# Four graph layers on one core: where the edges' order is checked, and how the edges are loaded

## The chip, the cores and the metric

The kernel runs on one core of a Trainium2 chip. A core has a matrix engine (TensorE, PE in the profile), a vector engine (VectorE, DVE), a scalar engine (ScalarE, ACT), GpSimd (POOL) and SyncE (SP), which work side by side, each through its own list of instructions in order. DMAs are issued from the lists of SP, ACT and POOL and carried out by 16 DMA engines. The metric is the device time of one execution in microseconds (us), as the median of several runs. One execution was also taken by the hardware profiler; its span and rows are what this text reads.

## The reference, cut to what matters

The graph has 3125 nodes with 128 features and 53,125 edges, given as `src`, `dst` and two edge types. Four layers follow each other, each with a residual and a layer norm:

```python
x = layernorm(x + L0(x, src, dst))                   # GIN, four times:  h = x + segment_sum(x[src], dst); relu(h@W1+b1)@W2+b2
x = layernorm(x + L1(x, src, dst, edge_type_8))      # a mean per relation
x = layernorm(x + L2(x, src, dst, edge_type_16))     # with attention per relation
x = layernorm(x + L3(x, src, dst, edge_type_8))      # gated
```

`setup_inputs` sorts the edges by `dst`. The reference itself does not depend on their order.

## The kernel before

**Two paths.** `any_order` is right for edges in any order. `in_order` is quicker and right only where the edges are sorted by `dst` and the destinations advance about evenly. `gnn_kernel` checks that first, and branches: `in_order` in the If, `any_order` in the Else.

**The edges as tiles.** 128 edges make a tile; there are TE = 416 tiles, the last with 5 edges. `gnn_kernel` loads each of the four edge arrays into a `raw` tile of 104 partitions (QR) by 4 by 128: partition q holds the tiles q, 104+q, 208+q and 312+q. Each array takes three DMAs: a first of 104 rows by three pieces of 512 bytes (L1170), a second of 103 rows of 512 bytes (L1171), and the five last edges (L1172). `dst` and `edge_type_8` are issued from SP, `src` and `edge_type_16` from ACT. Then two DMAs of single numbers fetch each tile's first and last destination (`lohi`, L1178 to L1180).

**The check and the places.** VectorE turns the arrays into floats (L1190), computes the tests (`bad`, `inner`, L1194 to L1217), and two small matmuls sum them to `flag` (L1219 to L1221). Then it computes, for each edge, where it belongs: `mod` (the source within its block of 128) and `kb` (block and destination, together), with `rel`, `k8` and the types for later layers. TensorE transposes seven such arrays (L1241), so that a tile becomes a column of 128 partitions; they are copied out of PSUM (L1242) and stored to DRAM as `keys` and `srcs` (L1245 to L1247). All engines then wait and branch on `flag` (L1248, L1250).

**The build of the adjacency matrix.** `gin_layers` loads `keys` back as `places` (L642), prepares the rows `offs` and `sto` (L654 to L662), and runs over the 416 tiles (L665). In each, VectorE makes two one-hot matrices `ohs` and `ohk` (L673, L675), TensorE multiplies them into the PSUM tile `pa` (L677, and L681 for the columns that the tile before left open), and ScalarE writes the result into `AT` in bf16 (L684). `pa` has three buffers, `ohs` four, `ohk` three. Each group of 8 tiles reads its offsets into registers first.

**What runs beside the build.** `first_parts(j)`, for j = 0 to 6, is called at the tiles 5, 14, ... 59 (L670). It loads 512 rows of `x` into `xn`, which has one buffer, and splits them into three bf16 parts `xs` on ScalarE and VectorE (`split`, L546). `dense(0, j)` multiplies `xs` with 512 columns of `AT` as soon as these are done (first after tile 73): one step of it, two matmuls, is run behind each tile (L685). After the build come the three further GIN steps, then layers 1 to 3, whose `edges` are loaded from `keys` at L694.

**What sets the order.** The order within an engine is made at build time by a scheduler that walks the program with modelled durations: an instruction keeps the rank of its place in the program, but a later one that its model finds ready while the engine is free goes ahead. On the chip each engine then keeps that order.

Of the kernel before, what the change touches and what calls it, by code (L numbers as in the profile page):

```python
# [21 lines left out]
F32 = mybir.dt.float32  # L22
# [7 lines left out]
P = 128  # L30
# [30 lines left out]
DRIFT = 40.0  # L61
PADDST = 4095
# [451 lines left out]
def gin_layers(ctx: ExitStack, tc: tile.TileContext, a: dict, pre: dict, outer: ExitStack, eps, srcI, xtab):  # L514
# [5 lines left out]
    ident, keys, lo, hi = (pre[k] for k in ("ident", "keys", "lo", "hi"))  # L520
# [3 lines left out]
    wk = ctx.enter_context(tc.tile_pool(name="g_wk", bufs=1, side="right"))  # L524
    xsd = [dram.tile([NP, 3, D], BF16, name=f"xsd{l}") for l in range(NL - 1)]

    AT = big.tile([P, NB, N + W], BF16, name="AT")

    xs = [big.tile([P, BPB if j < NCH - 1 else NB - BPB * (NCH - 1), 3, D], BF16, name=f"xs{j}") for j in range(NCH)]
    nc.vector.memset(xs[NCH - 1], 0.0)  # L530
    b1 = wk.tile([P, NL], F32, name="b1")
    with nc.allow_non_contiguous_dma(reason="a few columns"):
        nc.scalar.dma_start(b1, a["L0_gnn_b1"].rearrange("l o -> o l"))
# [85 lines left out]
    sp_pool = sp_ctx.enter_context(tc.tile_pool(name="g_parts", bufs=1, side="right"))  # L619
# [19 lines left out]
    weights(0)  # L639
    with tc.tile_pool(name="g_build", bufs=1) as bp, tc.tile_pool(name="g_hot", bufs=4) as hots:  # L640
        places = bp.tile([P, 2, TE], F32, name="places")
        nc.sync.dma_start(places, keys[:, :2, :])  # L642
        srcmod, keyb = places[:, 0, :], places[:, 1, :]
        nc.scalar.dma_start(srcI, pre["srcs"][:, :])
        iotah = bp.tile([P, NK], F16, name="iotah")
        nc.gpsimd.iota(iotah, pattern=[[1, NK]], base=0, channel_multiplier=0, allow_small_or_imprecise_dtypes=True)
        identh = bp.tile([P, P], BF16, name="identh")
        nc.vector.tensor_copy(identh, ident)


        regs = bp.tile([33, TE], I32, name="regs")
        row = bp.tile([1, TE], F32, name="row")
        offs, sto = regs[0:1, :], regs[32:33, :]
        nc.vector.tensor_copy(offs, lo)  # L654
        nc.vector.memset(row, 0.0)
        nc.vector.tensor_sub(row[:, 1:], hi[:, :FULL], lo[:, :FULL])
        nc.vector.tensor_scalar(row[:, 1:], row[:, 1:], -float(W), None, op0=OP.add)
        same = bp.tile([1, TE], F32, name="same")
        nc.vector.memset(same, 0.0)
        nc.vector.tensor_tensor(same[:, 1:], lo[:, 1:], hi[:, :FULL], OP.is_equal)  # L660
        nc.vector.tensor_tensor(row, row, same, OP.mult)
        nc.vector.tensor_scalar(sto, row, float(W), None, op0=OP.add)  # L662
        old = None
        under = []
        for t in range(TE):  # L665
# [4 lines left out]
            if t % 9 == 5 and t // 9 < NCH:  # L670
                first_parts(t // 9)
# [16 lines left out]
            for j in range(NCH):  # L688
                if t == last_tile(cols(j)[1]):
                    add_self(j)  # L690
                    under.append(dense(0, j, keep))
    ep = outer.enter_context(tc.tile_pool(name="f_edges", bufs=1))
    edges = ep.tile([P, 4, TE], F32, name="edges")
    nc.scalar.dma_start(edges, keys[:, 2:, :])  # L694
# [453 lines left out]
def gnn_kernel(ctx: ExitStack, tc: tile.TileContext, a: dict, out: bass.AP):  # L1148
    nc = tc.nc
    pp = ctx.enter_context(tc.tile_pool(name="pre", bufs=1))  # L1150
    dram = ctx.enter_context(tc.tile_pool(name="pre_dram", bufs=1, space=bass.MemoryType.DRAM))
    R8 = a["L1_gnn_W"].shape[0]
    keys = dram.tile([P, 6, TE], F32, name="keys")
    srcs = dram.tile([P, TE], I32, name="srcs")
    lo = pp.tile([1, TE], F32, name="lo")
    hi = pp.tile([1, TE], F32, name="hi")
    flag = pp.tile([1, 1], I32, name="flag")
    ident = pp.tile([P, P], F32, name="p_ident")
    iota = pp.tile([P, 2 * P], F32, name="p_iota")
    ones = pp.tile([P, P], F32, name="p_ones")  # L1160
    with (tc.tile_pool(name="pre_psum", bufs=1, space=bass.MemoryType.PSUM) as psum,
          tc.tile_pool(name="pre_tmp", bufs=1) as tmp):

        raw = {}
        for n, (name, pad) in enumerate((("dst", PADDST), ("src", 0), ("edge_type_8", 0), ("edge_type_16", 0))):
            eng = (nc.sync, nc.scalar)[n % 2]
            r = raw[name] = tmp.tile([QR, 4, P], I32, name="raw_" + name)
            nc.vector.memset(r[96:QR, 3, :], pad)
            e = a[name]
            eng.dma_start(r[:, :3, :], e[:3 * QR * P].rearrange("(k q p) -> q k p", q=QR, p=P))  # L1170
            eng.dma_start(r[:QR - 1, 3, :], e[3 * QR * P:FULL * P].rearrange("(q p) -> q p", p=P))  # L1171
            eng.dma_start(r[QR - 1:QR, 3, :LASTN], e[FULL * P:].rearrange("(q p) -> q p", q=1))  # L1172
        lohi = tmp.tile([1, 2, TE], I32, name="lohi")
        e = a["dst"]
        with nc.allow_non_contiguous_dma(reason="the tiles' first and last destinations"):
            firsts = bass.AP(tensor=e.tensor, offset=e.offset, ap=[[1, 1], [P, TE]])
            lasts = bass.AP(tensor=e.tensor, offset=e.offset + P - 1, ap=[[1, 1], [P, FULL]])
            nc.sync.dma_start(lohi[:, 0, :], firsts)  # L1178
            nc.scalar.dma_start(lohi[:, 1, :FULL], lasts)
            nc.scalar.dma_start(lohi[:, 1, FULL:], e[E - 1:E].rearrange("(a o) -> a o", a=1))  # L1180
        make_identity(nc, ident)
        nc.gpsimd.iota(iota, pattern=[[1, 2 * P]], base=0, channel_multiplier=0,
                       allow_small_or_imprecise_dtypes=True)
        nc.vector.memset(ones, 1.0)


        f = {}
        for name in raw:
            f[name] = tmp.tile([QR, 4, P], F32, name="f_" + name)
            nc.vector.tensor_copy(f[name], raw[name])  # L1190
        nc.vector.tensor_copy(lo, lohi[:, 0, :])
        nc.vector.tensor_copy(hi, lohi[:, 1, :])
        bad = tmp.tile([1, 8, TE], F32, name="bad")
        nc.vector.memset(bad, 0.0)  # L1194
        nc.vector.tensor_tensor(bad[:, 0, :FULL], hi[:, :FULL], lo[:, 1:], OP.is_gt)
        span = tmp.tile([1, TE], F32, name="span")
        nc.vector.tensor_sub(span, hi, lo)
        nc.vector.tensor_scalar(bad[:, 1, :], span, float(W - 1), None, op0=OP.is_gt)
        nc.vector.tensor_scalar(bad[:, 2, :FULL], span[:, :FULL], 1.0, None, op0=OP.is_lt)
        drift = tmp.tile([1, TE], F32, name="drift")  # L1200
        nc.gpsimd.iota(drift, pattern=[[1, TE]], base=0, channel_multiplier=0,
                       allow_small_or_imprecise_dtypes=True)
        nc.vector.scalar_tensor_tensor(drift, drift, -float(N * P) / E, lo, op0=OP.mult, op1=OP.add)
        nc.vector.tensor_scalar(bad[:, 3, :], drift, DRIFT, None, op0=OP.is_gt)
        nc.vector.tensor_scalar(bad[:, 4, :], drift, -DRIFT, None, op0=OP.is_lt)

        step = tmp.tile([1, TE], F32, name="step")
        nc.vector.tensor_sub(step[:, :FULL], lo[:, 1:], lo[:, :FULL])
        nc.vector.tensor_scalar(bad[:, 5, :FULL], step[:, :FULL], float(W), None, op0=OP.is_gt)
        nc.vector.tensor_scalar(bad[:, 6, :1], lo[:, :1], 0.0, None, op0=OP.is_gt)  # L1210
        nc.vector.tensor_scalar(bad[:, 7, :1], lo[:, FULL:], float(N - W), None, op0=OP.is_lt)
        inner = tmp.tile([QR, 4, P - 1], F32, name="inner")
        nc.vector.tensor_tensor(inner, f["dst"][:, :, :P - 1], f["dst"][:, :, 1:], OP.is_gt)
        found = tmp.tile([QR, 1], F32, name="found")
        nc.vector.tensor_reduce(found, inner, AX.XY, OP.add)
        rows = tmp.tile([1, 1], F32, name="rows")
        nc.vector.tensor_reduce(rows, bad, AX.XY, OP.add)  # L1217
        ps = psum.tile([1, 1], F32, name="ps_found")
        nc.tensor.matmul(ps, ones[:QR, 0:1], found, start=True, stop=False)  # L1219
        nc.tensor.matmul(ps, ones[0:1, 0:1], rows, start=False, stop=True)  # L1220
        nc.vector.tensor_scalar(flag, ps, 0.0, None, op0=OP.is_equal)  # L1221


        rel = tmp.tile([QR, 4, P], F32, name="rel")
        nc.vector.tensor_tensor(rel, f["dst"], f["dst"][:, :, 0:1].to_broadcast([QR, 4, P]), OP.subtract)
        sbI = tmp.tile([QR, 4, P], I32, name="sbI")
        nc.vector.tensor_scalar(sbI, raw["src"], 7, None, op0=OP.arith_shift_right)
        sb = tmp.tile([QR, 4, P], F32, name="sb")
        nc.vector.tensor_copy(sb, sbI)
# [50 lines left out]
```

## Time and profile before

| | us |
|---|---|
| median of 3 runs (2367.03 to 2371.94) | 2369.75 |
| the profiled execution | 2367.41 |
| its span | 2365.6 |
| edges loaded, checked and stored, branch taken: ends | 39.2 |
| `places` landed | 43.1 |
| first tile written to `AT` | 45.7 |
| first matmul of `dense(0, 0)` | 111.3 |
| last tile written to `AT` | 344.6 |
| busy over the span: PE, DVE, ACT, POOL | 81%, 50%, 21%, 50% |

The span begins with the first instruction and ends with the last; 1.8 us of the profiled execution lie around it. A share of busy time is a mean over stages that have different limits, so each stage has to be read by itself. The stretch that the change touches is the first 111 us, and a few instructions at the end of the build and of the kernel.

### The profile page before, as it was taken

Reading aid. Unit: us, or ns where it says so; the run is one execution under the profiler, and the core shown is the slowest. Engines: PE = TensorE matmul, PEld = TensorE weight load, DVE = VectorE, ACT = ScalarE, POOL = GpSimd, SP = SyncE. Lnnn points to the kernel's source line nnn. Section 1 sums busy time; section 2 is a strip of 40 time slices with the busy share of each in tenths; the row PEclk is TensorE's granted clock in tenths of the full one; section 3 lists DMA queues with packets and bytes.
Section 4 is the critical chain, followed back from the end, with each engine's and each line's share of the span. In section 5 each row is a group of like instructions: output and inputs, shape, how many; then the busy total and the mean of one; then the engine's idle time right before and its main releaser. Section 6 shows DMA issues by size and latency. Waiting matters only on the chain.

```text
span 2365.6 us, 37283 instructions
## 1 busy us (share of the span) xinstructions
PE 1921.5 (81%) x10848; PEld 1355.3 (57%) x10898; DVE 1172.6 (50%) x4724; ACT 492.3 (21%) x995; POOL 1194.0 (50%) x1259
## 2 busy tenths in 40 slices
PE   2698899999997899989786777777775778777777
PEld 1244344444445777777665666566664566666666
DVE  5677761121224656565554444455443455554554
ACT  1677761011104010000001222222222000000000
POOL 0000000000006777777774777777774777777774
PEclk8588889999995666676665656666665666767666
DMA  2000012020203222222221222222221222222221
GB/s 67 18 8 8 14 31 65 21 66 25 62 25 88 72 60 60 60 59 59 60 59 36 58 59 57 60 59 60 59 60 38 61 62 63 63 64 63 63 63 41
DMA packets 103154, 122.82 MB, mean 52 GB/s; under 512 B 25851, under 2 KB 82472, under 8 KB 102952
## 3 DMA queue, kind: packets, MB, share of 16 engines
q0 software_dynamic: 40000, 83.59, 14.6%
q1 hardware_dynamic: 51006, 28.49, 4.1%
q10 hardware_dynamic: 11946, 8.27, 1.2%
q8 instruction: 100, 1.64, 0.3%
q14 instruction: 102, 0.84, 0.1%
HBM read 104.98 MB, written 15.27 MB: 51 GB/s over the span
## 4 chain that ended last, share of the span: by engine, by line
PE 57%; issue 13%; DMA 12%; POOL 11%; DVE 6%; ACT 2%; DVEq 0%; SPq 0%; POOLq 0%; ACTq 0%
PE acc L595 16%; PE pw L1005 13%; POOL xg L908 11%; PE pm L1029 8%; DMA xg<-fx,f_srcI 6%; PE pc L1013 5%; PE pa L677 4%; PE pr L1050 3%; DMA xg<-gtab,f_srcI 3%; PE pr L603 1%; PE pr L610 1%; DVE sums L1007 1%; PE pa L681 1%; DMA xn<-in_x_dram 1%; DVE ohk L675 1%
## 5 line engine op out<-in xcount | busy, mean ns | idle before, releaser
L908 POOL DMA_INDIRECT xg<-fx,f_srcI x832 | 795.9, 957 | 934.9 <-DMA f_ggb<-in_L_gnn_gate_bias_dram 681.7
L1005 PE MATMUL pw<-oh,xg 128*128 128x128 f32 x2496 | 664.9, 399 | 180.8 <-DMA xg<-fx,f_srcI 83.6
L1005 PEld LDWEIGHTS pw<-oh,xg 128*128 128x128 f32 x2496 | 505.1, 271 | 291.7 <-DVE sums L1007 131.2
L1007 DVE TENSOR_TENSOR sums<-pw,sums 128x128 f32 x1248 | 357.8, 287 | 361.6 <-PE pw L1005 328.7
L908 POOL DMA_INDIRECT xg<-gtab,f_srcI x416 | 394.4, 948 | 151.5 <-issue 104.5
L595 PE MATMUL acc<-AT,xs 128*128 128x512 bf16 (+1 forms) x2050 | 438.2, 355 | 5.2 <-DMA xs<-xsd 1.8
L595 PEld LDWEIGHTS <-xs 128*128 128x128 bf16 x2100 | 176.0, 99 | 197.0 <-issue 19.7
L684 ACT CAST AT<-pa 128x400 f32 x416 | 213.1, 512 | 54.4 <-PE pa L681 28.3
L677 PE MATMUL pa<-ohk,ohs 128*128 128x425 bf16 x416 | 170.4, 424 | 45.7 <-ACT AT L684 18.0
L1013 PE MATMUL pc<-hw,rg 128*8 128x16 f32 x1456 | 92.7, 183 | 95.2 <-DVE rg L985 67.5
L675 DVE TENSOR_SCALAR ohk<-iotah,places 128x425 bf16<-128x425 f16 x416 | 139.2, 335 | 55.6 <-PE pa L681 49.3
L803 ACT COPY sums<-f_zero 128x1024 f32<-128x1024 f32 x74 | 75.2, 1042 | 325.0 <-PE pm L1029 188.0
L1013 PEld LDWEIGHTS pc<-hw,rg 128*8 128x8 f32 x1456 | 65.5, 89 | 129.1 <-DVE rg L985 76.0
L998 DVE SCALAR_TENSOR_TENSOR oh<-f_dcol,edges,coef 128x128 f32<-128x128 f32 x416 | 137.5, 344 | 0.7 <-ACT coef L955 0.6
L1003 DVE TENSOR_SCALAR oh<-p_iota,edges,g 128x128 f32<-128x128 f32 x416 | 135.9, 354 | 0.2
L677 PEld LDWEIGHTS <-ohs 128*128 128x128 bf16 x416 | 42.0, 101 | 139.1 <-DVE ohk L675 88.3
L996 DVE TENSOR_SCALAR oh<-p_iota,edges 128x128 f32<-128x128 f32 x416 | 121.0, 298 | 0.3
L600 DVE COPY hT<-acc 128x512 f32<-128x512 f32 (+1 forms) x28 | 17.3, 619 | 194.2 <-PE acc L595 194.2
L985 DVE TENSOR_TENSOR rg<-h,xg 128x32 f32<-128x32 f32 x104 | 19.8, 190 | 175.9 <-DMA xg<-gtab,f_srcI 170.8
L673 DVE TENSOR_SCALAR ohs<-iotah,places 128x128 bf16<-128x128 f16 x416 | 102.8, 247 | 0.9 <-DMA places<-keys 0.8
L1029 PE MATMUL pm<-f_bases,sums 128*128 128x128 f32 x400 | 100.2, 438 | 0.8 <-DVE sums L1007 0.8
L681 PE MATMUL pa<-ohk,ohs 128*128 x415 | 92.7, 223 | 9.3 <-issue 8.1
(193 smaller groups left out, 1898.5 us busy)
## 6 DMA issues: line engine op xcount, KB each, us to landing
xg<-fx,f_srcI POOLq DMA_INDIRECT x832
xsd<-sp SPq DMA_DIRECT2D x18, 384.0 KB
xg<-gtab,f_srcI POOLq DMA_INDIRECT x416
xs<-xsd SPq DMA_DIRECT2D x9, 384.0 KB
xs<-xsd ACTq DMA_DIRECT2D x9, 384.0 KB
xb<-fx SPq DMA_DIRECT2D x49, 64.0 KB
gtab<-yg SPq DMA_DIRECT2D x25, 68.0 KB
fx<-y SPq DMA_DIRECT2D x25, 64.0 KB
```

What stands on the lines that cost most here:

```text
L595: nc.tensor.matmul(acc[:, :n], xs[s // BPB][:, s % BPB, i, :], AT[:, s, c0:c1], start=s == 0 and i == 0, stop=s == NB - 1 and i == 2)
L675: nc.vector.tensor_scalar(ohk, iotah, keyb[:, t:t + 1], None, op0=OP.is_equal)
L677: nc.tensor.matmul(ps, ohs, ohk, start=True, stop=t == 0)
L684: nc.scalar.copy(AT[:, :, bass.ds(og[t % GRP], W)], ps3[:, :, :W])
L908: nc.gpsimd.indirect_dma_start(out=dst, out_offset=None, in_=table, in_offset=bass.IndirectOffsetOnAxis(ap=idx, axis=0))
L996: nc.vector.tensor_scalar(oh, iota[:, :W * NR], key8[:, u:u + 1], None, op0=OP.is_equal)
L998: nc.vector.scalar_tensor_tensor(oh.rearrange("p (d b) -> p d b", b=NR), W2["dcol"], dlr[:, u:u + 1], cgroups[u - u % GRP][:, u % GRP, :]. ...
L1003: nc.vector.tensor_scalar(oh, iota[:, :W * NR], key8[:, u:u + 1], gate, op0=OP.is_equal, op1=OP.mult)
L1005: nc.tensor.matmul(ps, x[:, u % 4, :D], oh, start=True, stop=True)
L1007: nc.vector.tensor_tensor(w, ps, w, OP.add)
L1013: nc.tensor.matmul(segs[j][:, bass.ds(spot[i][u], W)], r, hw[:, u % GRP, :], start=False, stop=u == last_tile(min(N, (j + 1) * P)))
L1029: nc.tensor.matmul(pb, s[:, r, :], w[:, r, :], start=False, stop=r == NR - 1)
```

## The change

`gnn_kernel` keeps no check of its own. It calls `in_order` without a branch, and at the very end reads `flag`, now the other way round, and runs `any_order` over the output if the edges were not in order:

```diff
-    good = nc.values_load(flag[0:1, 0:1], min_val=0, max_val=1)
-    with tc.If(good > 0) as cmp:
-        in_order(tc, a, out, pre)
-    with cmp.Else():
+    in_order(tc, a, out, pre)
+    bad = nc.values_load(pre["flag"][0:1, 0:1], min_val=0, max_val=1)
+    with tc.If(bad > 0):
         any_order(tc, a, out)
```

The loads and the places move into `gin_layers`. A partition now holds four tiles that follow each other, so an array takes one DMA of 103 rows of 2048 bytes and one of the rest:

```diff
-            nc.vector.memset(r[96:QR, 3, :], pad)
-            eng.dma_start(r[:, :3, :], e[:3 * QR * P].rearrange("(k q p) -> q k p", q=QR, p=P))
-            eng.dma_start(r[:QR - 1, 3, :], e[3 * QR * P:FULL * P].rearrange("(q p) -> q p", p=P))
-            eng.dma_start(r[QR - 1:QR, 3, :LASTN], e[FULL * P:].rearrange("(q p) -> q p", q=1))
+        nc.vector.memset(r[96:QR], pad)
+        rest = E - (QR - 1) * 4 * P
+        flat = r.rearrange("q k p -> q (k p)")
+        eng.dma_start(flat[:QR - 1, :], e[:(QR - 1) * 4 * P].rearrange("(q p) -> q p", q=QR - 1))
+        eng.dma_start(flat[QR - 1:QR, :rest], e[(QR - 1) * 4 * P:].rearrange("(q p) -> q p", q=1))
```

The tiles' first and last destinations are picked out by nine small matmuls with the identity instead of a DMA. Only `kb` and `mod` are transposed before the loop, in the buffers of `pa`, and copied straight into `places`:

```diff
+    def turn(dst, r, copy):
+        pt = psum.tile([P, NK], F32, name="pa", bufs=3)
+        for k in range(4):
+            nc.tensor.transpose(pt[:, k * QR:(k + 1) * QR], r[:, k, :], ident[:QR, :QR])
+        copy(dst.rearrange("p (q k) -> p k q", k=4), pt[:, :TE].rearrange("p (k q) -> p k q", k=4))
...
+    turn(keyb, kb, nc.scalar.copy)
+    turn(srcmod, mod, nc.vector.tensor_copy)
```

The first destinations are clipped to the band that the path can bear (`lo`, `offs`, `sto`), so that the path runs without harm on any edges. The other arrays are turned inside the loop, at the tiles in `LATE`, and stored to DRAM from ACT:

```diff
+LATE = [4, 5, 6, 7, 8, 10]
...
+    def later(i, r):
+        t = tmp.tile([P, TE], F32, name="turned", bufs=2)
+        turn(t, r, nc.scalar.copy)
+        nc.scalar.dma_start(keys[:, i, :], t)
+    def late(i):
+        if i == 0:
+            turn(turnedI, f["src"], nc.vector.tensor_copy)
+            nc.scalar.dma_start(srcs[:, :], turnedI)
+        elif i == 1:
+            later(0, rel)
+        elif i == 2:
+            t8 = fl("edge_type_8", sb)
+            later(3, t8)
+        elif i == 3:
+            nc.vector.scalar_tensor_tensor(mod, rel, float(R8), f["edge_type_8"], op0=OP.mult, op1=OP.add)
+            later(1, mod)
+        elif i == 4:
+            later(2, fl("edge_type_16", kb))
+        elif i == 5:
...
+            nc.vector.tensor_tensor(inner, flat[:, :4 * P - 1], flat[:, 1:], OP.is_gt)
+            nc.vector.tensor_reduce(found, inner, AX.X, OP.add)
+            tmp_ctx.close()
```

(`fl` casts a raw array to float on VectorE, here into the buffers of `sb` and `kb`.) The memory of these arrays is that of `xs` and of the working tiles afterwards. So `room()` makes these at tile 10, with a memset of the last `xs`; `b1`, the first weights and `srcI` are loaded there, and `first_parts` is called at the tiles 23, 32, ... 77:

```diff
-            if t % 9 == 5 and t // 9 < NCH:
-                first_parts(t // 9)
+            if t in LATE:
+                late(LATE.index(t))
+            if t == LATE[-1]:
+                wk = room()
...
+                weights(0)
+                nc.scalar.dma_start(srcI, srcs[:, :])
+            if t > LATE[-1] and t % 9 == 5 and t // 9 - 2 in range(NCH):
+                first_parts(t // 9 - 2)
```

The remaining tests (`checks`: some 20 VectorE instructions on one row of 416 numbers, a reduction and two matmuls into `flag`) stand behind the loop, ahead of the load of `edges`.

More of the change, by code (lines that the diff above doesn't have):

```diff
@@ L519, in gin_layers @@
     NL = a["L0_gnn_W1"].shape[0]
-    ident, keys, lo, hi = (pre[k] for k in ("ident", "keys", "lo", "hi"))
+    R8 = a["L1_gnn_W"].shape[0]
+    ident, iota, ones, flag = (pre[k] for k in ("ident", "iota", "ones", "flag"))
     dram = ctx.enter_context(tc.tile_pool(name="g_dram", bufs=1, space=bass.MemoryType.DRAM))
@@ L523, in gin_layers @@
     big = ctx.enter_context(tc.tile_pool(name="g_big", bufs=1, side="right"))
-    wk = ctx.enter_context(tc.tile_pool(name="g_wk", bufs=1, side="right"))
+    keep_ctx = ExitStack()
+    keep_ = keep_ctx.enter_context(tc.tile_pool(name="g_keep", bufs=1))
     xsd = [dram.tile([NP, 3, D], BF16, name=f"xsd{l}") for l in range(NL - 1)]
+    keys = dram.tile([P, 4, TE], F32, name="keys")
+    srcs = dram.tile([P, TE], I32, name="srcs")
     AT = big.tile([P, NB, N + W], BF16, name="AT")
-    xs = [big.tile([P, BPB if j < NCH - 1 else NB - BPB * (NCH - 1), 3, D], BF16, name=f"xs{j}") for j in range(NCH)]
@@ L530, in gin_layers @@
[L530 to L533, printed above, removed]
+    places = keep_.tile([P, 2, TE], F32, name="places")
+    srcmod, keyb = places[:, 0, :], places[:, 1, :]
+    iotah = keep_.tile([P, NK], F16, name="iotah")
+    identh = keep_.tile([P, P], BF16, name="identh")
+    regs = keep_.tile([33, TE], I32, name="regs")
+    offs, sto = regs[0:1, :], regs[32:33, :]
@@ new lines, in gin_layers @@
+    lo, hi = pre["lo"], pre["hi"]
+    found = keep_.tile([QR, 1], F32, name="found")
+    tmp_ctx = ExitStack()
+    tmp = tmp_ctx.enter_context(tc.tile_pool(name="g_tmp", bufs=1, side="right"))
+    raw, f = {}, {}
+    for n, (name, pad) in enumerate((("dst", PADDST), ("src", 0), ("edge_type_8", 0), ("edge_type_16", 0))):
+        eng = (nc.sync, nc.scalar)[n % 2]
+        r = raw[name] = tmp.tile([QR, 4, P], I32, name="raw_" + name)
+        nc.vector.memset(r[96:QR], pad)
+        e = a[name]
+        rest = E - (QR - 1) * 4 * P
+        flat = r.rearrange("q k p -> q (k p)")
+        eng.dma_start(flat[:QR - 1, :], e[:(QR - 1) * 4 * P].rearrange("(q p) -> q p", q=QR - 1))
+        eng.dma_start(flat[QR - 1:QR, :rest], e[(QR - 1) * 4 * P:].rearrange("(q p) -> q p", q=1))
@@ new lines, in gin_layers @@
+    make_identity(nc, ident)
+    nc.gpsimd.iota(iotah, pattern=[[1, NK]], base=0, channel_multiplier=0, allow_small_or_imprecise_dtypes=True)
+    nc.gpsimd.iota(iota, pattern=[[1, 2 * P]], base=0, channel_multiplier=0, allow_small_or_imprecise_dtypes=True)
+    at = tmp.tile([1, TE], F32, name="at")
+    nc.gpsimd.iota(at, pattern=[[1, TE]], base=0, channel_multiplier=0, allow_small_or_imprecise_dtypes=True)
+    nc.vector.memset(ones, 1.0)
+    def turn(dst, r, copy):
[3 more added lines that the diff above has]
+        copy(dst.rearrange("p (q k) -> p k q", k=4), pt[:, :TE].rearrange("p (k q) -> p k q", k=4))
@@ new lines, in fl @@
+    def fl(name, into=None):
+        f[name] = into if into is not None else tmp.tile([QR, 4, P], F32, name="f_" + name)
+        nc.vector.tensor_copy(f[name], raw[name])
+        return f[name]
+    fl("dst")
+    lohi = psum.tile([P, 2, BANK], F32, name="pr", bufs=1)
+    for i, c in enumerate((0, P - 1)):
+        for k in range(4):
+            m = QR - (i == 1 and k == 3)
+            nc.tensor.matmul(lohi[0:1, i, k * QR:k * QR + m], f["dst"][:, k, c:c + 1], ident[:QR, :m], start=True, stop=True)
@@ new lines, in gin_layers @@
+    nc.tensor.matmul(lohi[0:1, 1, TE - 1:TE], f["dst"][:, 3, LASTN - 1:LASTN], ident[:QR, QR - 1:QR], start=True, stop=True)
+    fl("src")
+    rel = tmp.tile([QR, 4, P], F32, name="rel")
+    nc.vector.tensor_tensor(rel, f["dst"], f["dst"][:, :, 0:1].to_broadcast([QR, 4, P]), OP.subtract)
+    sbI = tmp.tile([QR, 4, P], I32, name="sbI")
+    nc.vector.tensor_scalar(sbI, raw["src"], 7, None, op0=OP.arith_shift_right)
+    sb = tmp.tile([QR, 4, P], F32, name="sb")
+    nc.vector.tensor_copy(sb, sbI)
@@ new lines, in gin_layers @@
+    kb = tmp.tile([QR, 4, P], F32, name="kb")
+    nc.vector.scalar_tensor_tensor(kb, sb, float(WK), rel, op0=OP.mult, op1=OP.add)
+    mod = tmp.tile([QR, 4, P], F32, name="mod")
+    nc.vector.scalar_tensor_tensor(mod, sb, -float(P), f["src"], op0=OP.mult, op1=OP.add)
+    turn(keyb, kb, nc.scalar.copy)
+    turn(srcmod, mod, nc.vector.tensor_copy)
+    nc.vector.tensor_copy(identh, ident)
+    dst0 = keep_.tile([1, 2, TE], F32, name="dst0")
+    for i in range(2):
+        nc.scalar.copy(dst0[:, i, :].rearrange("o (q k) -> o k q", k=4), lohi[0:1, i, :TE].rearrange("o (k q) -> o k q", k=4))
@@ new lines, in gin_layers @@
+    nc.vector.tensor_scalar(at, at, float(N * P) / E, -DRIFT, op0=OP.mult, op1=OP.add)
+    nc.vector.tensor_tensor(lo, dst0[:, 0, :], at, OP.max)
+    nc.vector.tensor_scalar(at, at, 2 * DRIFT, None, op0=OP.add)
+    nc.vector.tensor_tensor(lo, lo, at, OP.min)
+    nc.vector.tensor_scalar(offs, lo, 0.0, float(N - 1), op0=OP.max, op1=OP.min)
+    nc.vector.tensor_copy(lo, offs)
+    nc.scalar.copy(hi, dst0[:, 1, :])
+    row = tmp.tile([1, TE], F32, name="row")
+    nc.vector.memset(row, 0.0)
+    same = tmp.tile([1, TE], F32, name="same")
@@ new lines, in gin_layers @@
+    nc.vector.memset(same, 0.0)
+    nc.vector.tensor_sub(row[:, 1:], hi[:, :FULL], lo[:, :FULL])
+    nc.vector.tensor_scalar(row[:, 1:], row[:, 1:], -float(W), None, op0=OP.add)
+    nc.vector.tensor_tensor(same[:, 1:], lo[:, 1:], hi[:, :FULL], OP.is_equal)
+    nc.vector.tensor_tensor(row, row, same, OP.mult)
+    nc.vector.tensor_scalar(row, row, float(W), 0.0, op0=OP.add, op1=OP.max)
+    nc.vector.tensor_scalar(sto, row, float(W), None, op0=OP.min)
+    def later(i, r):
+        t = tmp.tile([P, TE], F32, name="turned", bufs=2)
+        turn(t, r, nc.scalar.copy)
+        nc.scalar.dma_start(keys[:, i, :], t)
@@ new lines, in gin_layers @@
+    turnedI = tmp.tile([P, TE], I32, name="turnedI")
+    def late(i):
[13 more added lines that the diff above has]
+        elif i == 5:
+            flat = f["dst"].rearrange("q k p -> q (k p)")
+            inner = f["src"].rearrange("q k p -> q (k p)")[:, :4 * P - 1]
+            nc.vector.tensor_tensor(inner, flat[:, :4 * P - 1], flat[:, 1:], OP.is_gt)
+            nc.vector.tensor_reduce(found, inner, AX.X, OP.add)
+            tmp_ctx.close()
@@ new lines, in checks, with add @@
+    def checks(own):
+        first, last = dst0[:, 0, :], dst0[:, 1, :]
+        bad = own.tile([1, TE], F32, name="bad")
+        nc.vector.memset(bad, 0.0)
+        w = own.tile([1, TE], F32, name="bad_w")
+        def add(n, x, bound, op):
+            nc.vector.tensor_scalar(x, x, bound, None, op0=op)
+            nc.vector.tensor_tensor(bad[:, :n], bad[:, :n], x, OP.add)
+        nc.vector.tensor_sub(w[:, :FULL], last[:, :FULL], first[:, 1:])
+        add(FULL, w[:, :FULL], 0.0, OP.is_gt)
+        nc.vector.tensor_sub(w, last, first)
+        add(TE, w, float(W - 1), OP.is_gt)
+        nc.vector.tensor_sub(w, last, first)
+        add(FULL, w[:, :FULL], 1.0, OP.is_lt)
+        nc.vector.tensor_sub(w[:, :FULL], first[:, 1:], first[:, :FULL])
+        add(FULL, w[:, :FULL], float(W), OP.is_gt)
+        nc.vector.tensor_sub(w, first, lo)
+        add(TE, w, 0.0, OP.not_equal)
+        nc.vector.tensor_copy(w[:, 0:1], first[:, 0:1])
+        add(1, w[:, 0:1], 0.0, OP.is_gt)
+        nc.vector.tensor_copy(w[:, 0:1], first[:, FULL:])
+        add(1, w[:, 0:1], float(N - W), OP.is_lt)
+        rows = own.tile([1, 1], F32, name="rows")
+        nc.vector.tensor_reduce(rows, bad, AX.X, OP.add)
+        ps = psum.tile([P, NK], F32, name="pa", bufs=3)
+        nc.tensor.matmul(ps[0:1, 0:1], ones[:QR, 0:1], found, start=True, stop=False)
+        nc.tensor.matmul(ps[0:1, 0:1], ones[0:1, 0:1], rows, start=False, stop=True)
+        nc.vector.tensor_scalar(flag, ps[0:1, 0:1], 0.0, None, op0=OP.is_gt)
@@ L535, in cols, with room @@
+    late_ctx = {}
+    xs = []
+    def room():
+        late_ctx["xs"] = ctx.enter_context(tc.tile_pool(name="g_xs", bufs=1, side="right"))
+        late_ctx["wk"] = ctx.enter_context(tc.tile_pool(name="g_wk", bufs=1, side="right"))
+        xs.extend(late_ctx["xs"].tile([P, BPB if j < NCH - 1 else NB - BPB * (NCH - 1), 3, D], BF16, name=f"xs{j}")
+                  for j in range(NCH))
+        nc.vector.memset(xs[NCH - 1], 0.0)
+        return late_ctx["wk"]
     def cols(j):
@@ L618, in gin_layers @@
     sp_ctx = ExitStack()
-    sp_pool = sp_ctx.enter_context(tc.tile_pool(name="g_parts", bufs=1, side="right"))
     def keep(l, j, pr, rows, nb):
@@ L636, in back @@
                 "(b p) i d -> p b i d", p=rows))
[L639 to L662, printed above, removed]
+    with tc.tile_pool(name="g_hot", bufs=4) as hots:
         old = None
@@ L669, in gin_layers @@
                 sg = values(sto[:, t:t + n], PE, [(0, W)] * n)
-            if t % 9 == 5 and t // 9 < NCH:
-                first_parts(t // 9)
+            if t in LATE:
+                late(LATE.index(t))
+            if t == LATE[-1]:
+                wk = room()
+                b1 = wk.tile([P, NL], F32, name="b1")
+                with nc.allow_non_contiguous_dma(reason="a few columns"):
+                    nc.scalar.dma_start(b1, a["L0_gnn_b1"].rearrange("l o -> o l"))
+                weights(0)
+                nc.scalar.dma_start(srcI, srcs[:, :])
+                sp_pool = sp_ctx.enter_context(tc.tile_pool(name="g_parts", bufs=1, side="right"))
+            if t > LATE[-1] and t % 9 == 5 and t // 9 - 2 in range(NCH):
+                first_parts(t // 9 - 2)
             ohs = hots.tile([P, P], BF16, name="ohs")
@@ L691, in gin_layers @@
                     under.append(dense(0, j, keep))
+    with tc.tile_pool(name="g_checks", bufs=1) as own:
+        checks(own)
+    keep_ctx.close()
     ep = outer.enter_context(tc.tile_pool(name="f_edges", bufs=1))
     edges = ep.tile([P, 4, TE], F32, name="edges")
-    nc.scalar.dma_start(edges, keys[:, 2:, :])
+    nc.scalar.dma_start(edges, keys[:, :, :])
     for stages in under:
@@ L1150, in gnn_kernel @@
     pp = ctx.enter_context(tc.tile_pool(name="pre", bufs=1))
[L1151 to L1167, printed above, removed]
-            nc.vector.memset(r[96:QR, 3, :], pad)
-            e = a[name]
-            eng.dma_start(r[:, :3, :], e[:3 * QR * P].rearrange("(k q p) -> q k p", q=QR, p=P))
-            eng.dma_start(r[:QR - 1, 3, :], e[3 * QR * P:FULL * P].rearrange("(q p) -> q p", p=P))
-            eng.dma_start(r[QR - 1:QR, 3, :LASTN], e[FULL * P:].rearrange("(q p) -> q p", q=1))
[L1173 to L1229, printed above, removed]
-        mod = tmp.tile([QR, 4, P], F32, name="mod")
-        nc.vector.scalar_tensor_tensor(mod, sb, -float(P), f["src"], op0=OP.mult, op1=OP.add)
-        kb = tmp.tile([QR, 4, P], F32, name="kb")
-        nc.vector.scalar_tensor_tensor(kb, sb, float(WK), rel, op0=OP.mult, op1=OP.add)
-        k8 = tmp.tile([QR, 4, P], F32, name="k8")
-        nc.vector.scalar_tensor_tensor(k8, rel, float(R8), f["edge_type_8"], op0=OP.mult, op1=OP.add)
-        turned = tmp.tile([P, 6, TE], F32, name="turned")
-        turnedI = tmp.tile([P, TE], I32, name="turnedI")
-        for n, r in enumerate((mod, kb, f["src"], rel, k8, f["edge_type_16"], f["edge_type_8"])):
-            pt = psum.tile([P, TE], F32, name="pt", bufs=4)
-            for k in range(4):
-                nc.tensor.transpose(pt[:, k * QR:(k + 1) * QR], r[:, k, :], ident[:QR, :QR])
-            (nc.vector.tensor_copy if n % 2 == 0 else nc.scalar.copy)(
-                turnedI if n == 2 else turned[:, n - (n > 2), :], pt)
-            if n == 1:
-                nc.sync.dma_start(keys[:, :2, :], turned[:, :2, :])
-        nc.sync.dma_start(srcs[:, :], turnedI)
-        nc.scalar.dma_start(keys[:, 2:, :], turned[:, 2:, :])
@@ L1248, in gnn_kernel @@
-    good = nc.values_load(flag[0:1, 0:1], min_val=0, max_val=1)
-    pre = {"ident": ident, "iota": iota, "ones": ones, "keys": keys, "srcs": srcs, "lo": lo, "hi": hi}
-    with tc.If(good > 0) as cmp:
-        in_order(tc, a, out, pre)
-    with cmp.Else():
+    pre = {
+        "ident": pp.tile([P, P], F32, name="p_ident"),
+        "iota": pp.tile([P, 2 * P], F32, name="p_iota"),
+        "ones": pp.tile([P, P], F32, name="p_ones"),
+        "lo": pp.tile([1, TE], F32, name="lo"),
+        "hi": pp.tile([1, TE], F32, name="hi"),
+        "flag": pp.tile([1, 1], I32, name="flag"),
+    }
```

## The prediction

> **What bounds the kernel now.** I read the chain of waits over the first 50 us first, because the change rewrites what lies there. Columns: start, length, what.
>
> ```profile
> 1.43 10.98 DMA raw_src<-in_src_dram
> 12.43 5.24 DMA raw_edge_type<-in_edge_type_dram
> ...
> 18.20 0.36 DVE lo L1191
> ...
> 29.92 3.71 PE pt L1241 x20
> ...
> 35.59 3.44 DMA keys<-turned
> 39.34 3.79 DMA places<-keys
> 43.22 0.27 DVE ohs L673
> ```
>
> Three stretches set the start of the build: 17.9 us for the loads, 17.7 us of tests, places and transposes, and 7.6 us for the way to DRAM and back. The first tile reaches `AT` at 45.72.
>
> Second, the windows of the loads, since the change gives them another shape. Columns: stretch, length, busy time of five engines, clock, busy share of the 16 DMA engines, GB/s.
>
> ```profile
> 2.00:3.00 1.00, 0.00 (x0) 0.00 (x0) 0.69 (x1) 0.00 (x0) 0.02 (x1) 1.00 0.73 218
> ...
> 7.00:8.00 1.00, 0.00 (x0) 0.00 (x0) 0.00 (x0) 0.00 (x0) 0.00 (x0) 1.00 0.07 21
> 8.00:9.00 1.00, 0.00 (x0) 0.00 (x0) 0.16 (x1) 0.00 (x0) 0.00 (x0) 1.00 0.07 21
> 9.00:10.00 1.00, 0.00 (x0) 0.00 (x0) 0.27 (x1) 0.00 (x0) 0.00 (x0) 1.00 0.07 20
> ...
> 348.00:349.00 1.00, 1.00 (x7) 0.41 (x5) 0.00 (x0) 0.00 (x0) 0.00 (x0) 1.00 1.01 426
> ```
>
> The pieces of 104 rows (4 x 156 KB) are through by about 6 us. From 6 to 17 us the share is 0.07, one engine of sixteen, at 20 to 21 GB/s: some 0.2 MB, which is the four pieces of 103 rows (4 x 51.5 KB). They landed one after another: the casts started at 8.84, 12.74, 16.31 and 17.86.
>
> Third, what stands beside the early tiles, from the waits (us in total, times, longest):
>
> ```profile
> ACT xs L550 <- DMA xn<-in_x_dram: 27.8, 7, 9.9
> PE pa L677 <- ACT AT L684: 16.0, 9, 3.5
> ```
>
> From 45.2 to 87.1 ScalarE wrote only 32 tiles. Where nothing disturbs it, it writes 8 tiles in 4.58 us (336.21 to 340.79 in the timeline), 0.573 each, 18.3 for 32. So the seven `first_parts` cost 23.6 us. From 111.3 on TensorE is the bound (211.6 busy of 232.8), and everything later follows from when tile 73 is written.
>
> **The change, part by part.**
>
> *The loads.* Each array becomes 103 rows of 2048 B, 210.9 KB. Here a rule speaks against the change. The row first: 103 rows ran on one engine, 104 rows on about twelve (share 0.73). The Trainium skill, "DMA: Bandwidth & Descriptors", section "Why a DMA increments its semaphore by 16 and not by 1", gives the reason: the number of engines is the largest divisor, at most 16, common to the outer sizes of both patterns. 104 gives 13; 103 is prime and gives 1. The same page's rules for kernel authors ask for many small transfers to be joined into large ones; by that alone, on 16 engines at 20.5 GB/s, the four would move in 2.6 us. By the divisor they all queue on one engine. Its rate with rows of 2048 B is not in the trace: at least 20.7 GB/s (512 B rows above), at most 26.6 (426/16, `edges` with rows of 6656 B); I take the middle, 23.5, so 9.0 us for an array. The issue waits for a longer memset (about 1.2 us), bytes flow from about 2.3 (before: issue at 0.74, bytes just before 2.0), and the cast follows 0.8 behind the last byte (17.0 to 17.86). So dst lands at 12.1, src at 21.1, `edge_type_8` at 30.1, `edge_type_16` at 39.1.
>
> *The places.* Tests, `lohi` and the round trip through DRAM leave the path. `f_dst`, `rel`, the nine matmuls and the row work for `offs` and `sto` (some 5 us) fit between 12.1 and 21.1. Behind src stand f_src 0.43, sbI 0.33, sb 0.35, kb 0.60 and mod 0.60 (2.3), four transposes 0.9 (20 took 3.71), the copy 0.6, ohs and ohk 0.6, matmul and start of the eviction 0.7: 5.1, so the first tile at 26.2 instead of 45.72, **−19.5**.
>
> *The late arrays, on ScalarE.* ScalarE is the bound of the early tiles, so all of it counts: four copies of 0.51, five issues to `srcs` and `keys` of 0.38, and `b1`, two weights, `b2` and `srcI` at 0.43 to 0.53 (hidden until now under the load of `places`): 2.04 + 1.90 + 2.31 = **+6.25**. VectorE's share (about 3.7 us over seven tiles at some 0.5 each) lies beside it. Then `room()`: memset and weights wait until the last store has landed; `xn`, of like size, takes 2.8, and two tiles (1.15) cover part: **+1.65**. The first `xn` can be loaded only then, again 2.8 less 1.15: **+1.65**; before, that load fell under `places`.
>
> *`edge_type_16`.* Its cast stands in VectorE's order at tile 8, with every later `ohs` behind it, and so TensorE and ScalarE. Tile 8 comes up at 26.2 + 8 x 0.573 + 3.05 (ScalarE's share of the late work by then) = 33.8; the data come at 39.1: **+5.3**. That is with program order. But the scheduler moves work forward: `xs` of j = 6, called at tile 59, was run ahead of tile 30. If it puts the cast next to the first tile, then at 39.1 ten tiles (5.7), most late work (5.3) and waits of 2.2 are still to come: tile 11 at 52.3, against 45.7 + 6.3 = 52.0 before without `first_parts`.
>
> *`first_parts`.* Moved by 18 tiles in the program. Ends: 15 us gained, if the loads come well ahead and only ScalarE's 7 x 1.23 remain of 23.6, or nothing. I take nothing: one `xn` buffer, and a load of 2.8 to 3.4 us behind each split, stay as they are.
>
> *Checks and branch.* The 20 VectorE instructions (0.28 to 0.5, about 10 us) fall into 15.3 us in which VectorE idles after the build (345.3 to 360.6); without that cover they would delay the copy at 360.6. `edges`, queued on ACT behind them, is not needed before layer 1, and ACT's next work is at 362.5. Their two matmuls stand among TensorE's: 0 to 3 us, taken 1. At the end, a flag read and a branch after the last store: the If at the front cost 0.25 between landing (39.03) and the first instruction (39.28); the jump at the end exists already. 0 to 2, taken 0.5.
>
> Sum in program order: −19.5 + 6.25 + 1.65 + 1.65 + 5.3 + 1.5 = −3.1. With the cast up front: 52.3 − 52.0 + 1.5 = +1.8. Both happen in part; I take **−1**: 2366.4 for the profiled execution (2367.41). The median of the runs lies 2.3 higher, so 2368.7.
>
> **The rivals.**
>
> *The loads stay wide* (12 of 100). If rows of 2048 B are cut up across engines, all four land by some 6.5 us, as the 104-row pieces did by 6. The row work is then uncovered (3 us), the first tile comes at 14.6, `edge_type_16` is there in time: −31.1 + 9.55 + 1.5 = −20, 2349.7. For it: the GB/s of 2 to 6 us. Against it: the share of 0.07 for exactly such a row count.
>
> *Faster with narrow loads* (21 of 100). At 26.6 GB/s in program order: src at 19.0, the last type at 34.8, −21.6 + 9.55 + 3.1 + 1.5 = −7.5, 2362.3. Or `first_parts` overlaps better in its new place (up to −15, 2354).
>
> *The single engine becomes the bound of the build* (30 of 100; slower). With the cast up front the change is (landing of `edge_type_16`) − 37.3. At 20.7 GB/s it lands at 43.9: +6.6, 2376.3. The point from which it loses more than 0.2% is 42.0 us, a rate under 21.7 GB/s. For it: the only such rate in the trace is 20.7, and forward moves are the scheduler's habit. Against it: rows four times as long.
>
> *No measurable change* is my forecast, 37 of 100. A measurement of this kernel can tell 0.2%, 4.7 us, from nothing.
>
> **How the numbers follow.** The forecast's own range is 2364 to 2374. The fast cases together have 0.33 and the slow one 0.30. Leaving out the wide loads and the far slow tail (both costs at their upper ends and TensorE waiting 3 us on the checks: +11) gives 2354 to 2380.
>
> **What would show it.** In the profile after: a DMA share of 0.06 to 0.07 from about 2 to 38 us; the casts of dst, src and the types about 9 us apart; the first write to `AT` near 26; an idle VectorE ahead of the cast of `edge_type_16`; tile 73 and `dense(0, 0)` within some 5 us of 111; unchanged lengths after that. A share near 1 in the first 6 us and a first write near 15 would prove me wrong on the loads; `first_parts` without ScalarE waits of 3 us would on that part.

## The result, and the profile after

The time went from 2367.03 us (median of 15 runs, 2362.01 to 2371.94) to 2376.35 (15 runs, 2371.98 to 2380.36): a ratio of 1.0040, with a 95% interval of 1.0032 to 1.0048. The change is 9.3 us slower where −1 was forecast. The profiled execution after has a span of 2378.3, against 2365.6.

The windows of the loads in the profile after have the columns of those shown before:

```profile
4.00:6.00 2.00, 0.00 (x0) 0.00 (x0) 0.24 (x1) 0.00 (x0) 0.00 (x0) 1.00 0.07 26
...
14.00:16.00 2.00, 0.00 (x0) 0.00 (x0) 0.00 (x0) 0.00 (x0) 0.00 (x0) 1.00 0.07 26
...
34.00:36.00 2.00, 0.00 (x0) 0.00 (x0) 0.83 (x3) 0.00 (x0) 0.00 (x0) 1.00 0.07 25
```

A share of 0.07 is one busy DMA engine of sixteen: from 4 to 37 us, at 24 to 26 GB/s. There is no wide stretch any more like that of 2 to 6 us before. It is what the divisor rule of the Trainium skill ("DMA: Bandwidth & Descriptors", section "Why a DMA increments its semaphore by 16 and not by 1") gives for 103 rows.

The timeline of VectorE and ScalarE in the same profile shows what waited for that engine. Columns: start, length, engine, line, operation, output and input; in brackets the idle time before and what ended it. (L571 casts an array to float, L567 copies a transposed one out of PSUM, L602 copies `dst0`, L604 to L619 are the row work for `offs` and `sto`, L832 is the write to `AT`, L554 the issue of the DMA of an array's last edges.)

```profile
10.12 16.51 ACTq L554 DMA_DIRECT2D raw_edge_type<-in_edge_type_dram  x1
17.95 0.43 DVE L571 CAST f_dst<-raw_dst 104x512 f32<-104x512 int32 x1 [13.71 <-DMA raw_dst<-in_dst_dram]
...
23.85 0.43 DVE L571 CAST f_src<-raw_src 104x512 f32<-104x512 int32 x1 [4.74 <-DMA raw_src<-in_src_dram]
...
25.72 0.68 DVE L592 SCALAR_TENSOR_TENSOR mod<-sb,f_src 104x512 f32<-104x512 f32 x1
...
27.96 1.60 ACT L602 COPY dst<-pr 1x416 f32<-1x416 f32 x2
...
34.87 0.43 DVE L571 CAST sb<-raw_edge_type 104x512 f32<-104x512 int32 x1 [8.47 <-DMA raw_edge_type<-in_edge_type_dram]
...
37.88 0.43 DVE L571 CAST kb<-raw_edge_type 104x512 f32<-104x512 int32 x1 [2.18 <-DMA raw_edge_type<-in_edge_type_dram]
38.22 0.57 DVE L604 TENSOR_TENSOR lo<-dst,at 1x416 f32<-1x416 f32 x1
38.72 0.87 DVE L567 COPY places<-pa 128x416 f32<-128x416 f32 x1
...
41.90 0.51 ACT L832 CAST AT<-pa 128x400 f32 x1 [11.27 <-DVE ohk L823]
...
44.34 0.37 DVE L619 TENSOR_SCALAR regs<-row 1x416 int32<-1x416 f32 x1
...
46.02 1.06 ACT L832 CAST AT<-pa 128x400 f32 x2 [3.61 <-PE pa L829]
```

`mod` is ready for TensorE at 26.4. The two casts of the edge types, called in the program at the tiles 6 and 8, stand in VectorE's list ahead of the copy of `srcmod` into `places`, and they wait for the last two arrays. So the first tile, which needs neither type, is written at 41.90, only 3.8 us earlier than before. Of the row work for `offs` and `sto`, VectorE has all but one instruction (L603, between the casts) behind both, and ends it at 44.7. Tile 0 needs only `offs`; tile 1 is the first that needs `sto`, and it is written at 46.0.

The marks of each profiled execution, in us, with the times of the runs. Each ratio is to the kernel before on the same chip, whose median was 2364.35 to 2367.34; so kernels are best compared by their ratios.

| kernel | first write to `AT` | `dense(0, 0)` starts | from there to the end of the span | median | ratio to before (95%) |
|---|---|---|---|---|---|
| before | 45.7 | 111.3 | 2254.3 | 2367.03 | |
| after | 41.9 | 123.3 | 2255.0 | 2376.35 | 1.0040 (1.0032 to 1.0048) |
| e1_wide | 13.7 | 91.7 | 2255.2 | 2349.01 | 0.9926 (0.9913 to 0.9940) |
| e2_hold | 32.5 | 111.1 | 2258.2 | 2368.70 | 1.0005 (0.9996 to 1.0013) |
| e3_before_wide | 37.0 | 102.0 | 2250.5 | 2357.37 | 0.9964 (0.9950 to 0.9978) |
| e4_types_narrow | 25.9 | 103.5 | 2255.6 | 2361.32 | 0.9976 (0.9967 to 0.9984) |
| e5_quarter | 20.5 | 97.8 | 2251.9 | 2354.39 | 0.9950 (0.9936 to 0.9963) |
| e6_wide_hold | 13.7 | 91.3 | 2251.8 | 2345.41 | 0.9915 (0.9901 to 0.9928) |
| e7_wide_xn2 | 13.7 | 83.4 | 2249.8 | 2335.23 | 0.9872 (0.9857 to 0.9887) |
| e8_hold_sp | 27.5 | 106.0 | 2253.1 | 2363.34 | 0.9997 (0.9989 to 1.0006) |

What lies behind `dense(0, 0)` differs between these single executions by up to 8.4 us, without a trend. The gains and losses that the ratios show arise ahead of it. The execution of the kernel after in this table took 2380.08, 3.7 over its median, so its 12.0 us at `dense(0, 0)` may overstate a loss of 9.3. The clock that TensorE was granted does not explain the stretch ahead of it: in e1_wide it was 1.00 from 13 to 80 us, in e4_types_narrow 0.66 from 30 to 60 and 0.50 from 60 to 90, and from the first write to `dense(0, 0)` the two took 78.0 and 77.6.

### The profile page after: what moved, and what is told of

Read it like the earlier page. It is cut to its first block, busy times and chain, and to the rows that moved or that the text cites. A ratio compares the mean times of both kernels' runs of the same rounds, so it can differ in the third digit from the quotient of the medians.

```text
span 2378.3 us, 37309 instructions
## 1 busy us (share of the span) xinstructions
PE 1923.9 (81%) x10866; PEld 1355.0 (57%) x10916; DVE 1172.8 (49%) x4736; ACT 495.9 (21%) x1000; POOL 1195.1 (50%) x1259
## 4 chain that ended last, share of the span: by engine, by line
PE 50%; POOL 14%; issue 14%; DMA 13%; DVE 5%; ACT 2%; ACTq 0%; DVEq 0%; SPq 0%; POOLq 0%
PE acc L757 15%; POOL xg L1059 14%; PE pw L1156 11%; PE pm L1180 7%; DMA xg<-fx,f_srcI 7%; PE pc L1164 4%; PE pa L825 4%; DMA xg<-gtab,f_srcI 3%; PE pr L1201 3%; DMA raw_edge_type<-in_edge_type_dram 1%; PE pr L765 1%; PE pr L772 1%; ACT AT L832 1%; DMA xn<-in_x_dram 1%; PE pa L829 1%
## 5 line engine op out<-in xcount | busy, mean ns | idle before, releaser
L832 ACT CAST AT<-pa 128x400 f32 x416 | 213.3, 513 | 73.7 <-PE pa L829 32.0
L1164 PE MATMUL pc<-hw,rg 128*8 128x16 f32 x1456 | 91.7, 183 | 99.5 <-DVE rg L1136 69.8
```

Of the source, the lines that this page charges most:

```text
L832: nc.scalar.copy(AT[:, :, bass.ds(og[t % GRP], W)], ps3[:, :, :W])
L1164: nc.tensor.matmul(segs[j][:, bass.ds(spot[i][u], W)], r, hw[:, u % GRP, :], start=False, stop=u == last_tile(min(N, (j + 1) * P)))
```

## The experiments

**Wide loads.** The 103 full rows are loaded as 96 and 7, everything else as after:

```diff
-        eng.dma_start(flat[:QR - 1, :], e[:(QR - 1) * 4 * P].rearrange("(q p) -> q p", q=QR - 1))
+        eng.dma_start(flat[:96, :], e[:96 * 4 * P].rearrange("(q p) -> q p", q=96))
+        eng.dma_start(flat[96:QR - 1, :], e[96 * 4 * P:(QR - 1) * 4 * P].rearrange("(q p) -> q p", q=QR - 97))
```

> The kernel after, but each edge array's 103 full rows are loaded as 96 rows and 7 rows. Queue theory (one DMA engine carries 844 KB, the last array lands at 37.8 us, and the first tiles wait for it): 96 rows spread over 16 engines, all four arrays land by about 7 us, the first write to AT comes near 17 instead of 41.9, and the time falls by about 25 us to 2351 us. Rival (the late arrays, the copies on ScalarE and the freeing of memory inside the loop eat what the front gains): the first write comes earlier, but tile 73 and dense(0,0) move by less than 10 us, and the time stays above 2366 us.

2349.01 us, where the queue theory had 2351. The windows of this kernel:

```profile
2.00:3.00 1.00, 0.00 (x0) 0.00 (x0) 0.89 (x3) 0.00 (x0) 0.46 (x2) 1.00 0.99 332
3.00:4.00 1.00, 0.00 (x0) 0.00 (x0) 0.85 (x4) 0.00 (x0) 0.00 (x0) 1.00 1.07 295
```

All sixteen engines are busy, and the four arrays are in by about 6 us. In the kernel after the same bytes took from about 2 to 37 us through one engine. The casts of the types stand in the same place in VectorE's list, and now find their data there: no wait stands before them in the timeline of this kernel:

```profile
8.82 0.43 DVE L572 CAST sb<-raw_edge_type 104x512 f32<-104x512 int32 x1
...
9.63 0.43 DVE L572 CAST kb<-raw_edge_type 104x512 f32<-104x512 int32 x1
...
13.67 0.51 ACT L833 CAST AT<-pa 128x400 f32 x1 [2.79 <-DVE ohk L824]
```

The rival of this run is refuted: against the kernel after, the first write came 28.2 us earlier, and `dense(0, 0)`, behind tile 73, 31.6.

**The casts kept in their place.** Loads as after, one edge for the scheduler:

```diff
             if t in LATE:
-                late(LATE.index(t))
+                with tc.issue_after(hot.ins):      # hot: the ohk of the tile before
+                    late(LATE.index(t))
```

> The kernel after with its narrow loads, but the late pieces may not be moved ahead of the tiles at which they are called (an order edge on VectorE). Order theory (the two casts of the types stand ahead of the copy of places in VectorE's order, and so everything waits for the last load): the first write to AT comes near 34 instead of 41.9 and the time falls by 6 to 8 us, to about 2369 us. Queue theory alone (the late work needs the last array at 37.8 anyway): at most 3 us, about 2374 us.

2368.70 us, as the order theory had it, and no longer to be told from before. The timeline of VectorE and ScalarE in this kernel:

```profile
29.30 0.87 DVE L567 COPY places<-pa 128x416 f32<-128x416 f32 x1
...
32.48 0.51 ACT L833 CAST AT<-pa 128x400 f32 x1 [1.89 <-DVE ohk L824]
...
37.81 0.42 DVE L571 CAST sb<-raw_edge_type 104x512 f32<-104x512 int32 x1
...
41.25 0.42 DVE L571 CAST kb<-raw_edge_type 104x512 f32<-104x512 int32 x1
```

The copy of `places` goes ahead, the first write comes 9.4 us earlier than after, and the casts, now at their tiles, wait for nothing. So of the 27 us that lie between the kernel after and wide loads (2376.35 less 2349.01), about 8 (2376.35 less 2368.70) are gained by the order alone. The other 20 are left with the casts in place: `src` is cast at 23.77 here, and at 6.24 in e1_wide.

**The kernel before with its 103-row pieces cut into 96 and 7**, the same edit at its second DMA:

> The kernel before, with the second DMA of each edge array (103 rows of 512 B) cut into 96 and 7 rows. Queue theory: the window of 6 to 17 us with one busy engine goes, the casts of the types end near 10 us instead of 18, about 8 us less: 2359 us. If the row count is not the cause: no change, 2367 us.

2357.37 us: the old kernel too lost some 8 to 10 us to this row count (8.5 by the ratio, 10.0 by the medians). It also gives the fair comparison for the change: with wide loads on both sides, 2349.01 against 2357.37, the change is worth about 8 us.

**Only the types narrow:** `dst` and `src` as in e1_wide, the types as after.

> The kernel after with wide loads for dst and src (96 and 7 rows) and the narrow loads left for the two types. Order and queue together: the types land near 12 and 21 us, their casts still stand ahead of the copy of places, so the first write to AT comes near 25 us: about 17 us less than the kernel after, 2359 us, some 8 us more than with all four loads wide. If only the loads of dst and src mattered: as with four wide loads, 2351 us.

2361.32 us. Timeline of this kernel:

```profile
19.25 0.43 DVE L575 CAST sb<-raw_edge_type 104x512 f32<-104x512 int32 x1 [10.83 <-DMA raw_edge_type<-in_edge_type_dram]
...
21.86 0.43 DVE L575 CAST kb<-raw_edge_type 104x512 f32<-104x512 int32 x1 [1.77 <-DMA raw_edge_type<-in_edge_type_dram]
...
25.88 0.51 ACT L836 CAST AT<-pa 128x400 f32 x1 [11.71 <-DVE ohk L827]
```

`dst` and `src` are cast by 6.3 us, and the first write still waits for the types: 12.2 us later than with four wide loads, the 12.2 by which the last cast is later (21.86 less 9.63). This is the wait of the kernel after by itself.

**The new tiles, loaded in the row counts of before** (104 rows of 1536 B, 103 of 512 B, the last five edges):

> The kernel after, with four tiles to a row as in the change, but each array loaded in the row counts of the kernel before: 104 rows of 1536 B, 103 rows of 512 B and the last five edges. Queue theory: the one engine carries 4 x 52.7 KB again, the types land near 11 and 14 us, the first write to AT comes near 19 us, the time is about 2353 us, 23 less than the kernel after. If the new arrangement of the tiles in itself cost the time: about 2376 us.

2354.39 us. The arrangement of four tiles to a row is not what costs. Loading all four tiles of a row by one DMA of 103 rows, rather than only one of the four, costs about 21 us (1.0040 less 0.9950).

**Wide loads and the order edge together:**

> Wide loads and the order edge together. Order theory: the place of the casts costs only while their data are late, so with wide loads the edge is worth nothing: 2349 us within 2 us. If the casts' place cost by itself: about 8 us less than with wide loads alone, 2341 us.

2345.41 us, between the two expectations. In the profile `dense(0, 0)` starts at 91.3, against 91.7 with wide loads alone, so this stretch gained 0.4. The rest of the 2.6 us between the two ratios lies behind it, where executions differ by more, and the intervals of the two ratios overlap. Whether the edge is worth anything once the data are early was not settled; the 8 us that it was worth with late data it is not.

**Two buffers for `xn`,** on top of wide loads:

> Wide loads, and two buffers for xn in place of one. If the seven first_parts are held by the landing of a load that can be issued only when the single buffer is free (2.7 to 3.9 us of ScalarE idle at each): the loads run one ahead, dense(0,0) starts 10 to 15 us earlier, 2337 us. If the stretch is bound by ScalarE's or VectorE's own work there: 2349 us.

2335.23 us, ratio 0.9872 (0.9857 to 0.9887): the quickest version here, ahead of both kernels. The waits of ScalarE for `xn` up to 125 us (total, times, longest), in the kernel after, with wide loads alone, and in this one:

```profile
ACT xs L712 <- DMA xn<-in_x_dram: 19.8, 7, 3.9
```

```profile
ACT xs L713 <- DMA xn<-in_x_dram: 17.7, 7, 3.3
```

```profile
ACT xs L713 <- DMA xn<-in_x_dram: 8.6, 6, 2.6
```

The second buffer takes 9.1 of the 17.7 us, and `dense(0, 0)` starts 8.3 earlier than with one, less than the 10 to 15 expected.

**All four narrow loads from SP,** with the order edge:

> Narrow loads and the order edge, as before (2368.7 us), but all four arrays are issued from SP, so that ScalarE is not held in the issue of a load until 26.6 us. VectorE's list is the same instruction for instruction. If the row work for offs and sto runs late because ScalarE was held (it makes dst0, on which that work waits): dst0 is there by about 23, the first write to AT comes about 2 us earlier, and the time falls by about 2 us. If it runs late because VectorE's list has it behind mod anyway: the first two tiles move by less than 2 us and the time stays at 2368.7 within 2 us.

2363.34 us, 0.9997 (0.9989 to 1.0006), against 1.0005 for e2_hold: the intervals overlap, so the time doesn't decide. The profile does tell the two apart, and shows something that neither expectation had:

```profile
12.16 0.43 DVE L571 CAST f_dst<-raw_dst 104x512 f32<-104x512 int32 x1 [7.92 <-DMA raw_dst<-in_dst_dram]
...
20.57 0.43 DVE L571 CAST f_src<-raw_src 104x512 f32<-104x512 int32 x1 [7.26 <-DMA raw_src<-in_src_dram]
...
23.63 0.58 DVE L604 TENSOR_TENSOR lo<-dst,at 1x416 f32<-1x416 f32 x1
...
27.47 0.51 ACT L833 CAST AT<-pa 128x400 f32 x1 [2.66 <-DVE ohk L824]
```

From one queue the arrays come one after another, 8.4 us apart, where two queues shared the engine and brought `dst` at 17.95 and `src` at 23.85. The first write comes 5.0 us earlier than in e2_hold: 3.2 of it from `src` (20.57 against 23.77). In e2_hold VectorE also waited 2.06 for `dst0`; here `lo` starts without that wait. But `lo` still stands behind `mod`, though `dst0` was there from 16.6 on: that part is VectorE's list, which is the same in both.

## Why the prediction was wrong

**Right: one engine.** 103 rows ran on one DMA engine, as the divisor rule and the 0.07 of the trace before said. Its rate was 24 to 26 GB/s, the upper part of the range taken (20.7 to 26.6), so the last cast came at 37.88, near the 39.1 of the prediction. Cutting the rows was worth 27 us (e1_wide against after).

**Wrong in form: one after another.** `dst` at 12.1 and `src` at 21.1 are what a single queue gives (12.16 and 20.57 in e8_hold_sp). The kernel issues from two, and `dst` landed 6 us late, `src` 3. A page of the Trainium skill ("DMA: Bandwidth & Descriptors", section "SWDGE vs HWDGE vs iDMA", under "Issuing engines are not separate DMA queues") says just that: DMAs of several issuers interleave on the same engines.

**The step that failed** is "Both happen in part; I take −1". The prediction gave two places of the `edge_type_16` cast, at tile 8 or next to the first tile, and took a middle. Both casts of the types went wholly to the front, past the copy of `places`, most of the row work and the first `ohs`. That is the order of the program as built, the same with early data (e1_wide); why the scheduler chose it was not looked into.

The case "with the cast up front" was priced too low as well. By the measured landing its own formula gives +0.6 (37.9 − 37.3); the runs gave +9.3. The case has tile 11 at 52.3. It was written at 62.0, as the twelfth write of the profile after:

```profile
62.01 1.05 ACT L832 CAST AT<-pa 128x400 f32 x2
```

The 9.7 between them are:

- −1.2: the last cast came at 37.88, not at 39.1.
- +8.1: from that cast to tile 1, which the case counts at nothing. The prediction had the row work done between 12.1 and 21.1, and the copy of `places` right behind src. But in VectorE's list the copy of `places` and almost all of the row work stand behind the cast, and run to 44.7. In e1_wide, where no type is waited for, the same stretch is as long (9.63 to 17.78).
- +2.8: from tile 1 to tile 11, 16.0 instead of 13.2.

Pinning the casts took the wait for the types off the first tiles and gave back about 8 us. It did not take the row work away: in e2_hold too tile 1 comes 4.1 us behind tile 0. So the case in program order, −3.1, did not hold either where e2_hold ran it (1.0005): its first tile was written at 32.5, not at 26.2, and its wait of 5.3 for `edge_type_16` did not come up.

**Near, in part by luck: the late work.** Between the first write and `dense(0, 0)` lie 65.6 us before and 78.0 with wide loads, where no type is waited for. That is 12.4 more, where the prediction had 9.55 for the late work. But 2.6 of them lie between tile 0 and tile 1 (4.1 instead of 1.5), where the row work now stands. The writes of tiles 0 and 1 before, and of tile 1 in e1_wide (tile 0 at 13.67, shown above):

```profile
45.72 0.51 ACT L684 CAST AT<-pa 128x400 f32 x1 [0.53 <-DVE ohs L673]
47.22 0.51 ACT L684 CAST AT<-pa 128x400 f32 x1 [0.99 <-PE pa L681]
```

```profile
17.78 1.06 ACT L833 CAST AT<-pa 128x400 f32 x2 [3.60 <-PE pa L830]
```

From tile 1 on it is 9.8. The sum came out, but not each term: ScalarE's four copies of transposed arrays took 0.90 each, not 0.51 as before, 1.6 us more. Their output is now interleaved by four; whether that is the cause, and which terms were smaller than taken, was not tested.

**Right:** `first_parts` gained nothing by its new place (19.8 us of waits at seven, against 17.9 at the last six before), and the cause given, one `xn` buffer, accounts for about half of that wait (e7_wide_xn2). TensorE waited 0.42 for the matmul of the checks (taken 1). From the end of the last `y` to the end of the span it is 5.25, against 4.7 before (estimated 0.5 more). Neither checks nor branch matter.

**The rival that came true** is "the single engine becomes the bound of the build". Its mechanism was right and its point wrong: it was to lose more than 0.2% from a landing at 42.0 on. It landed at 37.9 and lost 0.4%, since 8.1 us of other work stood between that landing and tile 1.

## What to carry to other kernels

Look at the row count of a DMA, not only at its bytes: with 103 rows 0.2 MB an array ran on one engine of sixteen, and as 96 and 7 rows the same bytes were through in a few us. Work that is put later in the program is put later on the chip only if something holds it there: where a scheduler may move it, ask which load it waits for, and what stands behind it in the list. And price a case that looks bad in full, with all that its place puts behind the wait, before taking a mean with the good one: here that was 8.1 us.

## What the runs showed of the hardware

An engine that issues a DMA can be held by it. With narrow loads ScalarE was in one issue from 10.12 to 26.63, of the last edges of an array (1.6 KB), and SP in one of 16.39 us (4.13 to 20.52); with all four from SP, in one of 8.21 (e8_hold_sp). With wide loads no issue in the first 6 us took over 0.51. The section "Issuing engines are not separate DMA queues", named above, calls the time to issue usually small beside the DMA itself; here it was not. What holds the engine was not tested: it was only seen where one DMA engine had a long queue. In the kernel after the hold cost nothing: ScalarE's `dst0` was there at 29.6, and the row work that reads it was behind the cast at 37.88. In e2_hold it cost VectorE the 2.06.

On one DMA engine, rows of 2048 B moved at 24 to 26 GB/s, rows of 512 B at 20 to 21.
